# Routed blocks of 64 tokens: both halves of the hidden layer in one tile

## Chip, core and metric

The kernel runs on one NeuronCore of a Trainium2 chip. Times are device microseconds of one execution. The engines are named as in the profile: PE (TensorE matmuls), PEld (TensorE weight loads), DVE (VectorE), ACT (ScalarE), POOL (GpSimd) and SP (SyncE, which issues most DMAs).

## What is computed

The reference is one decoder layer on 2 x 2048 tokens of 512 channels: an attention with squared ReLU, a cross attention with 16 heads on a context of 128 tokens, and a feed-forward layer with a shared expert and 32 routed experts. Only the routed experts matter here. Every token goes to the expert with the largest gate logit, scaled by that logit's sigmoid:

```python
order = jnp.argsort(topk_ids)
sorted_x = xs[order]
g = _grouped_mm(sorted_x, routed_gate_w, tokens_per_expert)
u = _grouped_mm(sorted_x, routed_up_w, tokens_per_expert)
d = _grouped_mm(jax.nn.silu(g) * u, routed_down_w, tokens_per_expert)
```

Each expert has weights of 512 x 1024 for `g` and `u` and 1024 x 512 for `d`, all in float32.

## The kernel before

Every float32 operand is split into two parts, `hi` on ACT (a cast to fp32r, line 93) and `lo` on DVE (the difference, line 96), and products are made as three terms, lo x hi, hi x lo and hi x hi.

The stage `routed` runs from about 1866 us to the end. The experts are ranked by their number of tokens, and each rank has a capacity, `CAP`: 448, 384, five of 256, four of 192, thirteen of 128, eight of 64. Each is cut into blocks of 256, 128 and 64 tokens; this makes 13 blocks of 64. The experts run in groups: a large one, then one of 64 tokens and one of 128, later two of 128. Between them stand blocks of `Rest`, which is a part of the shared expert (lines 823 to 856).

`load` brings one matrix of an expert in eight pieces of 128 x 512 (`raw`), and splits each into `rh` (ACT) and `rl` (DVE). The pieces of `g` and `u` take turns in 48 buffers, those of `d` in 16. So a piece of a later expert can be split only when PE has done with the piece whose buffer it takes.

A block goes through these steps. `gather` fetches its rows (an indirect DMA of POOL, line 905). `turn` transposes them on PE (tile `pt`) and splits them (`th`, `tl`). `gate` and `up` make the products `g` and `u`. `turn_h` transposes the hidden layer (tile `ht`) and splits it (`th`, `tl`). `down` multiplies by `d` and adds the rows to the output with an indirect DMA (line 1019). The steps of neighbouring blocks are interleaved: a block's `turn_h` comes between the next block's `gate` and `up`, and its `down` comes after that `up`.

A block of 64 tokens has only 64 rows. Its turned input holds hi in columns 0 to 63 and lo in columns 64 to 127 of the same tile, so that one matmul gives the hi terms in partitions 0 to 63 of PSUM and the lo terms in partitions 64 to 127. `both` adds the two halves: ACT copies one of them to SBUF, DVE adds the other (lines 952 and 953). The hidden layer has 1024 columns, which are made in two halves of 512 (`n` = 0 and 1 in `up_product`). Each half of each block has an `s` tile of its own, of which the first 64 partitions are used. The product `s<-u,s` is made by POOL (line 969), and `turned` transposes each half in four pieces of 64 x 128 into a PSUM bank of its own (line 912).

The order of the instructions on each engine isn't written out: a planner with estimated durations and priorities orders them when the kernel is built, and every engine then runs its list in that order. PSUM banks come in four pairs; `g` uses P2, `u` P3, `ht` P4, `d` and `pt` P1.

Of the kernel before, what the change touches and what calls it, by code (L numbers as in the profile page):

```python
# [9 lines left out]
FR = mybir.dt.float32r  # L10
# [4 lines left out]
A = mybir.AluOpType  # L15
AF = mybir.ActivationFunctionType
# [6 lines left out]
C = 512  # L23
# [17 lines left out]
def f32(ap):  # L41
    return ap.bitcast(F32)
# [45 lines left out]
def split(g, hi, lo, src, lo_engine=None, hi_engine=None):  # L88

    if isinstance(lo_engine, cycle):  # L90
        lo_engine = next(lo_engine)
    if hi_engine is None:
        g.nc.scalar.copy(hi, src)  # L93
    else:
        hi_engine.tensor_copy(hi, src)
    (lo_engine or g.nc.vector).tensor_tensor(lo, src, f32(hi), A.subtract)  # L96
# [65 lines left out]
def three(terms):  # L162

    (wh, wl), (xh, xl) = terms
    return (wl, xh), (wh, xl), (wh, xh)
# [694 lines left out]
def routed(g, xs, rest, plan, idx, wg, wu, wd, out):  # L860
    nc = g.nc
# [8 lines left out]
    X, S, HT, W = {}, {}, {}, {}  # L870
# [38 lines left out]
    def turned(x, m, bank, tags):  # L909

        for k in range(4):
            nc.tensor.transpose(bank[:, k * m:(k + 1) * m], x[0:m, k * 128:(k + 1) * 128], g.ident[0:m, 0:m])
        hi = g.tile(tags[0], "th", FR, (128, 4, 128))
        if m == 64:
            split(g, hi[:, :, 0:64], hi[:, :, 64:128], bank[:, 0:256].rearrange("p (k n) -> p k n", k=4))
            return (hi,)
        lo = g.tile(tags[1], "tl", FR, (128, 4, 128))
        split(g, hi[:], lo[:], bank[:].rearrange("p (k n) -> p k n", k=4))
        return hi, lo
# [16 lines left out]
    def product(p, x, w):  # L936
        n, last = 0, len(x) * (1 + len(x[0][0])) - 1
        for (xk, k), wk in zip(x, w):
            terms = three((wk, xk)) if len(xk) == 2 else [(v, xk[0]) for v in wk[::-1]]
            for v, y in terms:  # L940
                nc.tensor.matmul(p[:], y[:, k, :], v, start=n == 0, stop=n == last)
                n += 1

    def up_product(b, r, which, tag):
        hi, lo = W[r][which]
        for n in range(2):
            p = g.bank(tag, which)
            product(p, [(X[b], k) for k in range(4)], [(hi[2 * k + n], lo[2 * k + n]) for k in range(4)])
            yield p

    def both(out, p):
        nc.scalar.copy(out, p[64:128])
        nc.vector.tensor_tensor(out, p[0:64], out, A.add)

    def gate(b, r, m):
        S[b] = []
        for p in up_product(b, r, "g", "P2"):
            s = g.tile("G", "s")
            if m == 64:
                both(s[0:64], p)  # L960
            nc.scalar.activation(s[0:m], s[0:64] if m == 64 else p[:], AF.Silu)
            S[b].append(s)

    def up(b, r, m):
        for s, p in zip(S[b], up_product(b, r, "u", "P3")):
            if m == 64:
                u = g.tile("D", "u")
                both(u[0:64], p)
                nc.gpsimd.tensor_tensor(s[0:64], u[0:64], s[0:64], A.mult)
            else:  # L970
                nc.vector.tensor_tensor(s[:], p[:], s[:], A.mult)

    def hidden(b, r, part):
        if part == 0:
# [19 lines left out]
            HT[b].append((hh, hl))  # L994

    def turn_h(b, r, m):
        if m < 256:
            HT[b] = [turned(s, m, g.bank("P4", "ht"), "CD") for s in S.pop(b)]

    def down(b, r, m):  # L1000
        h = HT.pop(b)
        hi, lo = W[r]["d"]
        for j in range(-(-m // 128)):
            o = g.bank("P1", "d")
            if m < 256:
                product(o, [(h[k // 4], k % 4) for k in range(8)], list(zip(hi, lo)))
            else:
                n = 0
                for k in range(8):
                    for w, y in three(((hi[k], lo[k]), h[k // 2])):  # L1010
                        nc.tensor.matmul(o[:], y[:, k % 2, j * 128:(j + 1) * 128], w, start=n == 0, stop=n == 23)
                        n += 1
            v = g.tile("I", "v")
            if m == 64:
                both(v[0:64], o)
            else:
                nc.scalar.copy(v[:], o[:])  # L1017
            rows = slice(0, min(m, 128))
            nc.gpsimd.indirect_dma_start(out=out, out_offset=bass.IndirectOffsetOnAxis(ap=idx[rows, b + j:b + j + 1], axis=0),  # L1019
                                         in_=v[rows], in_offset=None, bounds_check=T - 1, oob_is_err=False, compute_op=A.add)  # L1020
# [4 lines left out]
    for r in order:  # L1025
        at = 0
        while at < CAP[r]:
            m = next(m for m in (256, 128, 64) if at + m <= CAP[r])
# [14 lines left out]
    def first(b, r, m):  # L1043
        if r is None:
            rest.gate(b)
        elif m < 256:
            gate(b, r, m)
        else:
            hidden(b, r, 0)

    def second(b, r, m):
        if r is None:
            rest.up(b)
        elif m < 256:
            up(b, r, m)
        else:
            hidden(b, r, 1)

    def third(b, r, m):
        if r is None:  # L1060
            rest.down(b)
        else:
            down(b, r, m)
# [5 lines left out]
    def turn_hidden(b, r, m):  # L1069
        if r is not None:  # L1070
            turn_h(b, r, m)
# [7 lines left out]
    for i, block in enumerate(blocks):  # L1079
        b, r, m = block  # L1080
# [13 lines left out]
        if i > 0:  # L1094
            third(*blocks[i - 1])
            r = blocks[i - 1][1]
# [136 lines left out]
```

## Time and profile before

| what | value |
|---|---|
| median of 3 runs | 2747.65 us (2745.44 to 2748.27) |
| the profiled execution | 2744.97 us, of which the span is 2743.2 us |
| granted clock of TensorE | 0.997 |
| PE busy in the span | 2681.9 us |
| DVE, ACT, POOL busy | 2054.2, 1786.0, 1033.7 us |
| `s<-u,s` on POOL (line 969) | 26 instructions, 41.0 us |
| `s<-s` silu of 64 partitions (line 961) | 26 instructions, 16.4 us |
| `ht` transposes of 64 rows (line 912) | 104 instructions in 13 blocks |

A row of the timeline gives the start, the time until the last of the merged instructions ended, the engine, the line, the operation, the tiles (result <- operands), the shape and the number of instructions. Matmuls are pipelined: one that takes 0.39 us by its row can start 0.227 us after the one before it. What PE spends on a piece of work is therefore read from start to start. A row of the waits gives the engine and its tile and line, what it waited for, the sum in us, how often, and the longest.

### The profile page before, as it was taken

The numbers are of one execution on the slowest core, as the hardware profiler recorded it, in microseconds if no ns is written. First come the engines' busy times: TensorE is split into PE (matmuls) and PEld (weight loads), VectorE is DVE, ScalarE is ACT, GpSimd is POOL, SyncE is SP. The second block draws the span as 40 slices with busy tenths as digits, with TensorE's granted clock in tenths as the row PEclk, the third lists the DMA queues.
The fourth block names the chain that finished last, engine by engine and source line by source line (L and its number), as shares of the span: only waits on it lengthen the run. The fifth ranks groups of instructions, "written<-read, shape, count | busy, mean of one in ns | idle before, by whom it ended". The sixth has DMA issues, their size and how long they took to land. (4 is left out here: it accounts for less than half of the span.)

```text
span 2743.2 us, 47449 instructions
## 1 busy us (share of the span) xinstructions
PE 2681.9 (98%) x14788; PEld 2293.6 (84%) x14788; DVE 2054.2 (75%) x4671; ACT 1786.0 (65%) x3995; POOL 1033.7 (38%) x821
## 2 busy tenths in 40 slices
PE   7999999999999999999999999999999999999998
PEld 5877877777878999899997888888889888898886
DVE  8888788888887888888876722243777787778985
ACT  6777777787867777777775111133666676768885
POOL 5686566667653333333330030001223122223331
PEclk9999999999999999999999999999999999999999
DMA  4021112112120222322246222254888999899994
GB/s 141 32 70 70 70 62 72 64 58 81 36 70 33 75 90 90 114 78 91 74 138 207 96 93 101 72 173 109 271 265 277 284 302 298 280 279 287 325 316 140
DMA packets 237999, 396.69 MB, mean 145 GB/s; under 512 B 29376, under 2 KB 67280, under 8 KB 237744
## 3 DMA queue, kind: packets, MB, share of 16 engines
q1 hardware_dynamic: 223024, 366.45, 39.5%
q0 software_dynamic: 14720, 27.19, 5.0%
q8 instruction: 117, 1.92, 0.3%
q14 instruction: 138, 1.13, 0.1%
HBM read 311.67 MB, written 83.83 MB: 144 GB/s over the span
## 5 line engine op out<-in xcount | busy, mean ns | idle before, releaser
L96 DVE TENSOR_TENSOR rl<-raw,rh 128x512 fp32r<-128x512 f32 x768 | 510.5, 711 | 106.2 <-ACT rh L93 98.0
L93 ACT CAST rh<-raw 128x512 fp32r<-128x512 f32 x768 | 440.3, 622 | 135.7 <-DMA raw<-in_rg 82.8
L96 POOL TENSOR_TENSOR pl<-p,ph 128x512 fp32r<-128x512 f32 x320 | 427.4, 1344 | 242.9 <-ACT ph L93 219.0
L343 DVE TENSOR_TENSOR p<-s,rl 128x512 f32<-128x512 f32 x512 | 343.4, 683 | 81.5 <-ACT rl L341 62.0
L93 ACT CAST ph<-p 128x512 fp32r<-128x512 f32 x448 | 277.7, 622 | 153.9 <-DVE p L343 148.3
L341 ACT ACTIVATE rl<-s 128x512 f32<-128x512 f32 x512 | 301.3, 599 | 34.7 <-PE s L337 21.1
L1019 POOL DMA_INDIRECT out_dram<-v,idx x46 | 108.0, 2347 | 424.8 <-ACT v L1017 332.8
L448 ACT ACTIVATE e<-e,nm 128x128 f32<-128x128 f32 x512 | 199.2, 391 | 63.2 <-DVE nm L445 62.8
L451 POOL TENSOR_TENSOR e<-e,ri 128x512 f32<-128x512 f32 x128 | 133.5, 1043 | 245.2 <-DVE ri L449 128.3
L298 PE MATMUL o<-pl,vwh 128*128 128x512 f32 x512 | 208.0, 406 | 11.0 <-DVE pl L96 7.6
L337 PE MATMUL s<-qh,kwl 128*128 128x512 f32 x512 | 207.2, 406 | 7.3 <-DVE p L343 7.0
L337 PE MATMUL s<-qh,kwh 128*128 128x512 f32 x512 | 201.1, 393 | 0.0
L337 PE MATMUL s<-ql,kwh 128*128 128x512 f32 x512 | 201.1, 393 | 0.0
L298 PE MATMUL o<-ph,vwh 128*128 128x512 f32 x512 | 200.7, 392 | 0.0
L298 PE MATMUL o<-ph,vwl 128*128 128x512 f32 x512 | 198.8, 392 | 0.0
L96 DVE TENSOR_TENSOR pl<-p,ph 128x512 fp32r<-128x512 f32 x192 | 185.2, 965 | 16.1 <-ACT ph L93 13.7
L905 POOL DMA_INDIRECT x<-xs,idx x46 | 57.3, 1247 | 312.0 <-DMA raw<-in_rd 171.8
L93 ACT CAST hh<-s 128x512 fp32r<-128x512 f32 x92 | 57.0, 620 | 164.3 <-DVE s L760 117.2
L422 PE MATMUL q<-yh,wql 128*128 128x256 f32 x512 | 149.5, 292 | 2.8 <-DVE v L481 2.6
L422 PE MATMUL q<-yh,wqh 128*128 128x256 f32 x512 | 145.6, 284 | 0.0
L422 PE MATMUL q<-yl,wqh 128*128 128x256 f32 x512 | 145.0, 283 | 0.0
L755 PE MATMUL g<-z,sw 128*128 128x512 f32 x576 | 139.5, 390 | 1.7 <-ACT s L759 1.7
(296 smaller groups left out, 7607.9 us busy)
## 6 DMA issues: line engine op xcount, KB each, us to landing
raw<-in_rg SPq DMA_DIRECT2D x256, 256.0 KB, 5.3
raw<-in_ru SPq DMA_DIRECT2D x256, 256.0 KB, 5.1
raw<-in_rd SPq DMA_DIRECT2D x256, 256.0 KB, 4.7
z<-zT SPq DMA_DIRECT2D x128, 256.0 KB, 5.4
b<-x SPq DMA_DIRECT2D x64, 256.0 KB, 2.6
xt<-in_x SPq DMA_DIRECT2D x32, 256.0 KB, 2.7
x<-xt SPq DMA_DIRECT2D x32, 256.0 KB, 2.0
x<-b SPq DMA_DIRECT2D x32, 256.0 KB, 2.3
```

Source lines behind the costliest of these rows:

```text
L93: g.nc.scalar.copy(hi, src)
L96: (lo_engine or g.nc.vector).tensor_tensor(lo, src, f32(hi), A.subtract)
L298: nc.tensor.matmul(o[:], w, y[:], start=kt == 0 and n == 0, stop=kt == 15 and n == 2)
L337: nc.tensor.matmul(s[:], w, y[:], start=n == 0, stop=n == 2)
L341: m0 = nc.scalar.activation(r[:], s[:], AF.Relu)
L343: m1 = nc.vector.tensor_tensor(p[:], s[:], r[:], A.mult)
L422: nc.tensor.matmul(o[:, i, :], part(w, k, p), y[k // 2][:, k % 2, :], start=n == 0, stop=n == 11)
L448: nc.scalar.activation(e[:, hs], e[:, hs], AF.Exp, bias=nm[:, h:h + 1], scale=0.125, accum_out=su[:, h:h + 1])
L451: nc.gpsimd.tensor_tensor(e4, e4, ri[:].unsqueeze(2).to_broadcast([128, 4, 128]), A.mult)
L755: nc.tensor.matmul(p[:], part(w, k, c), y[k][:], start=n == 0, stop=n == 11)
L905: nc.gpsimd.indirect_dma_start(out=x[rows], out_offset=None, in_=xs, in_offset=bass.IndirectOffsetOnAxis(ap=idx[rows, b + j:b + j + 1], ax ...
L1019: nc.gpsimd.indirect_dma_start(out=out, out_offset=bass.IndirectOffsetOnAxis(ap=idx[rows, b + j:b + j + 1], axis=0), in_=v[rows], in_offse ...
```

## The change

For blocks of 64 tokens, the two halves of the hidden layer share one `s` tile: half 0 in partitions 0 to 63, half 1 in partitions 64 to 127. `both` takes the number of the half, and puts its result into those partitions. The silu is made once over 128 partitions after both halves are added. The `u` halves share a tile in the same way, and the product `s<-u,s` is made once, on DVE. `turn_h` transposes the common tile in four pieces of 128 x 128 into one bank. Each result has the first half's tokens in columns 0 to 63 and the second's in columns 64 to 127; two splits take them apart into the same two `th` tiles as before. `down` is the same. Blocks of 128 and 256 tokens do the same work as before, but the planner orders the whole stage anew.

```diff
-    def both(out, p):
-        nc.scalar.copy(out, p[64:128])
-        nc.vector.tensor_tensor(out, p[0:64], out, A.add)
+    def both(out, p, n=0):
+        at, other = slice(64 * n, 64 * n + 64), slice(64 - 64 * n, 128 - 64 * n)
+        nc.scalar.copy(out[at], p[other])
+        nc.vector.tensor_tensor(out[at], p[at], out[at], A.add)

     def gate(b, r, m):
         S[b] = []
-        for p in up_product(b, r, "g", "P2"):
-            s = g.tile("G", "s")
+        for n, p in enumerate(up_product(b, r, "g", "P2")):
             if m == 64:
-                both(s[0:64], p)
-            nc.scalar.activation(s[0:m], s[0:64] if m == 64 else p[:], AF.Silu)
-            S[b].append(s)
+                if n == 0:
+                    S[b].append(g.tile("G", "s"))
+                both(S[b][0], p, n)
+            else:
+                s = g.tile("G", "s")
+                nc.scalar.activation(s[:], p[:], AF.Silu)
+                S[b].append(s)
+        if m == 64:
+            nc.scalar.activation(S[b][0][:], S[b][0][:], AF.Silu)

     def up(b, r, m):
+        if m == 64:
+            u = g.tile("D", "u")
+            for n, p in enumerate(up_product(b, r, "u", "P3")):
+                both(u, p, n)
+            s = S[b][0]
+            nc.vector.tensor_tensor(s[:], u[:], s[:], A.mult)
+            return
         for s, p in zip(S[b], up_product(b, r, "u", "P3")):
-            if m == 64:
-                u = g.tile("D", "u")
-                both(u[0:64], p)
-                nc.gpsimd.tensor_tensor(s[0:64], u[0:64], s[0:64], A.mult)
-            else:
-                nc.vector.tensor_tensor(s[:], p[:], s[:], A.mult)
+            nc.vector.tensor_tensor(s[:], p[:], s[:], A.mult)
...
     def turn_h(b, r, m):
-        if m < 256:
+        if m == 64:
+            s, = S.pop(b)
+            bank = g.bank("P4", "ht", (128, 4, 2, 64))
+            for k in range(4):
+                nc.tensor.transpose(bank[:, k, :, :].rearrange("p n t -> p (n t)"), s[:, k * 128:(k + 1) * 128], g.ident)
+            HT[b] = []
+            for n in range(2):
+                h = g.tile("C", "th", FR, (128, 4, 128))
+                split(g, h[:, :, 0:64], h[:, :, 64:128], bank[:, :, n, :])
+                HT[b].append((h,))
+        elif m == 128:
             HT[b] = [turned(s, m, g.bank("P4", "ht"), "CD") for s in S.pop(b)]
...
             if m == 64:
-                both(v[0:64], o)
+                both(v, o)
```

## The prediction, made before the changed kernel ran

> **What bounds the kernel now.** I read the busy table of the page first, then the busy time by stretches, then what PE waits for in the routed stage, and last its timeline around the transposes that the change touches.
>
> ```profile
> PE 2681.9 (98%) x14788; PEld 2293.6 (84%) x14788; DVE 2054.2 (75%) x4671; ACT 1786.0 (65%) x3995; POOL 1033.7 (38%) x821
> 2100.00:2200.00 100.00, 99.54 (x589) 87.96 (x588) 73.32 (x116) 70.31 (x130) 23.15 (x17) 1.00 0.91 283
> 2500.00:2600.00 100.00, 99.70 (x500) 82.73 (x499) 92.09 (x147) 81.71 (x158) 33.77 (x19) 1.00 0.95 308
> ```
>
> The two lower lines are stretches of the routed stage (about 1866 us to the end); their columns are length, then PE, PEld, DVE, ACT, POOL busy, granted clock, DMA share, GB/s. PE is full to half a microsecond in a hundred while the DMA engines are at 0.91 to 0.95, DVE at 73 to 92%. A busy PE could hide waits, so I checked the pace: 512-column matmuls start every 0.227 us and 256-column ones every 0.12 us throughout. The waits put down to PE in the whole routed stage are small:
>
> ```profile
> PE d L941 <- ACT th L93: 1.0, 1, 1.0
> PE g L941 <- ACT th L93: 0.9, 1, 0.9
> PE g L941 <- DVE th L96: 0.7, 2, 0.4
> PE g L986 <- DVE tl L96: 0.7, 1, 0.7
> ```
>
> So in this stage a microsecond of PE work is a microsecond of kernel, unless PE then runs into its suppliers. What the change removes from PE is therefore read from start-to-start distances, not from busy time. Eight transposes of a 64-token block (64 rows in use), four of a full block, both between 512-column products:
>
> ```profile
> 2714.24 0.39 PE L941 MATMUL g<-rh,th 128*128 128x512 f32 x1
> 2714.56 0.71 PE L912 MATMUL ht<-ident,s 64*128 64x64 f32 x8
> ...
> 2715.54 0.39 PE L941 MATMUL u<-rh,tl 128*128 128x512 f32 x1
> 2467.15 0.39 PE L941 MATMUL g<-rh,th 128*128 128x512 f32 x1
> 2467.38 0.60 PE L912 MATMUL pt<-ident,x 128*128 128x128 f32 x4
> ...
> 2468.05 0.40 PE L941 MATMUL u<-rh,th 128*128 128x512 f32 x1
> ```
>
> Each distance holds two normal steps (0.454). The eight small ones cost 2715.54 - 2714.24 - 0.454 = 0.85 us, the four large ones 0.90 - 0.454 = 0.45 us. Four small ones alone cost 0.59 us by the same measure (the `pt` of these blocks), so a small one is about (0.85 - 0.59) / 4 = 0.065 us and going to 64 rows and back about 0.33 us.
>
> **What the Trainium skill says.** "TensorEngine Tiling (Array Packing)", Key Properties: changing the tiling mode, not only the tile, drains TensorE. The trace agrees: 0.33 us for a run of 64-row transposes whatever its length. "SBUF — State Buffer", Who interferes with whom: a DVE instruction with two SBUF inputs and a GpSimd instruction that reads SBUF exclude each other for a whole instruction. The trace agrees:
>
> ```profile
> L96 DVE TENSOR_TENSOR rl<-raw,rh x742: 669/682/2205, 1903.6 to 2727.9; 128x512 fp32r<-128x512 f32 x186
> L969 POOL TENSOR_TENSOR s<-u,s x26: 1279/1624/2275, 1910.9 to 2708.2; 64x512 f32<-64x512 f32 x26
> ```
>
> (min/median/max ns.) The weight splits normally take 682 ns; the 38 of them that overlap one of the 26 POOL products average 1265, so the products cost DVE 38 x 0.58 = 22 us. "VectorE: DVE Perf Modes", Two Vector instructions with no wait between them: an instruction whose operands start in another group of 32 partitions than those before is held until the earlier ones are done. Before, all of them start at partition 0, so no row shows it; I bound it below.
>
> **The change part by part.** There are 13 blocks of 64 tokens.
>
> PE, transposes of the hidden layer. Before: 8 of 64 rows per block; after: 4 of 128 rows, the form that the 128-token blocks use. In the trace 8 of the 13 blocks have one run beside full-row work (0.84 us each), 2 share the 64-row mode with a neighbouring `pt` (1.09 less the 0.59 that `pt` costs anyway: 0.50), 3 are cut into two runs of four (1.18, 1.25 and 1.19). Sum 6.7 + 1.0 + 3.6 = 11.3 us. After: 13 x 0.445 = 5.8. The compiled order shows one `pt` of 64 rows cut in two (three, eight matmuls, one): one more change of mode, +0.33. PE work: **-5.2 us**.
>
> DVE. The `both` additions stay (four per block, 0.68 each). The product `s<-u,s` comes from POOL, once over 128 partitions: +13 x 0.68 = +8.9 us, price of `hl<-s,hh`, which also reads two SBUF tiles. Lost port time returns, -22 us. Changes of start partition: rows run 0.68 long but start 0.60 apart, so a held one loses about 0.08, and four to eight per block make 4 to 8 us; neither end matters for the path, as DVE has 8% free in its fullest stretch. Net 5 to 13 us less.
>
> ACT. Copies stay; one silu of 128 partitions for two of 64: -13 x 0.63 = -8 us, off the path. POOL: -26 products, 41 us busy; gathers and scatters queued behind them go earlier. PE waits for no gather, so I count 0. The two splits per block read PSUM in pieces of 64 now, the same 256 elements: 0 to +0.1 us each on DVE, hidden under PE.
>
> Waits added. The silu now waits for the second addition too; behind it on ACT stand weight casts (`rh`), and PE waits for these. The product on DVE waits for the silu, and the weight splits queue behind it. The compiled order puts the silu by the copies of `u` and the product one to five entries after the last addition, so the silu is done when the product's turn comes: 0, covered by the `u` product of the same block on PE (16 x 0.227 = 3.6 us); up to 0.6 us for a split behind it if not. I paired each weight piece's split on DVE with the first matmul that reads it: nearly everywhere it is ready 5 us or more ahead. The exception is `u` of the 256-token experts: ready 0.1 to 0.6 us ahead at 2150, 2234, 2316 and 2399 us. There the order changes too. Before, DVE and ACT made both halves of that block's turned input (`th`, `tl`) between those splits; after, four of its eight transposes stand ahead, and one cast (0.5 to 0.6 us) and one `tl` (0.6) leave the queue before the weights. PE loses 0.8 to 1.2 us there per round (4.2 us in four rounds, from gaps in its starts). PE comes there no earlier relative to what frees the buffers: the 64-token `down` moves ahead with it. From -4.2 to +2 us in all; I take about a third of the possible gain: **-1.3 us**.
>
> Loads, stores and their order on SP are the same in number. The tail after the last weight load keeps its order (`ht` of the last 64 block, 24 `u`, 16 `d`, eight `ht`, 24 `d`): 0.
>
> Sum -6.5 us. The profiled execution took 2744.97 us (span 2743.2 plus 1.8 around it), 2.7 below the median of the three runs, 2747.65. So 2738.5 against its own time and 2741 against the median.
>
> **The rivals.**
> 1. *PE saves and then waits.* The tight loads follow ACT and DVE, not PE. If in the five rounds with a 256-token expert PE arrives 0.4 us earlier than its suppliers and in the last groups one of the lone waits (0.4 to 1.1 us) grows, 2 to 4 of the 5.2 us are given back: about 2745. For it: margins of 0.1 us. Against: DVE and ACT get lighter.
> 2. *Slower: the second half of the turned hidden layer is late.* In the compiled order its ACT cast and DVE subtraction stand behind weight splits, and in many blocks behind the product of the block between, so `down` becomes eight matmuls, a few of `g`, eight more. PE reaches the second eight 24 x 0.12 + 4 x 0.11 + 14 x 0.227 + 8 x 0.227 + 2 x 0.227 = 8.8 us after the transposes; DVE should have the half after about 2.9 + 0.3 + 0.7 + 0.4 = 4.3 us. It decides once DVE is 4.5 us behind; 2 us past that in eight blocks is +16, less 6: about 2757. Against: DVE is idle a quarter of the time where most of these blocks lie.
> 3. *DVE was worth more than its busy share says.* The 22 us that POOL held from it fall in bursts of about 1.7 us per block. If most of PE's short waits (some 8 us from the gaps in its starts) come from that backlog, 4 us more go: about 2737.
>
> That the change does not do what it says is ruled out: the compiled order shows 52 transposes of 128 x 128 where 104 stood, and 13 products on DVE.
>
> **How the numbers follow.** Forecast 0.60 (own range 2737 to 2744), rival 1 0.27, rival 2 0.08, rival 3 0.05. A measurement tells about 0.2% (5.5 us) from no change, so faster means below 2742.2. The forecast gives about 0.51 of its 0.60 to that side, rival 3 all, a little of rival 1: 0.57. Within 0.2%: 0.09 + 0.26 = 0.35. Slower: 0.08. The range 2734 to 2748 leaves out rival 2 and the ends.
>
> **What would show it.** Right: `ht` of 64 rows gone, each run of four full ones costing 0.45 us between starts; weight splits without values of 2.2 us; POOL 41 us less busy; PE busy some 5 us less, waits no larger. Rival 1: PE work down, waits on `rl`, `th` or `tl` up by the same. Rival 2: PE `d` waiting for DVE `th`. I am wrong if PE's starts around the new transposes cost 0.85 us as before, or if PE's waits grow by over 5 us.

## The result, and the profile after

The changed kernel took 2739.28 us (median of 11 runs, 2737.38 to 2742.28) against 2746.22 us for the kernel before (11 runs, 2742.96 to 2749.73). The ratio is 0.9975, with a 95% interval of 0.9966 to 0.9985: 0.25% faster, or 7 us.

Page and stretches of the changed kernel (columns as before the change):

```profile
PE 2677.5 (98%) x14736; PEld 2291.0 (84%) x14736; DVE 2046.0 (75%) x4684; ACT 1784.7 (65%) x3982; POOL 985.1 (36%) x795
2100.00:2200.00 100.00, 98.68 (x582) 87.33 (x581) 73.84 (x120) 70.80 (x130) 20.50 (x14) 1.00 0.90 280
2500.00:2600.00 100.00, 98.83 (x481) 81.42 (x480) 90.03 (x149) 81.16 (x155) 24.85 (x15) 1.00 0.96 309
```

PE has 52 matmuls fewer and is 4.4 us less busy. POOL is 48.6 us less busy, of which the products are 41. DVE is 8.2 us less busy although it makes 13 products more. But PE has more small gaps in both stretches than before (98.7 and 98.8 us of 100 instead of 99.5 and 99.7).

The timeline of PE at the last 64-token block, and the same measure as in the prediction: 2711.55 - 2710.65 - 0.454 = 0.45 us, where it was 0.85.

```profile
2710.65 0.39 PE L941 MATMUL g<-rh,th 128*128 128x512 f32 x1
2710.88 0.60 PE L1011 MATMUL ht<-ident,s 128*128 128x128 f32 x4
2711.23 0.48 PE L941 MATMUL u<-rl,th 128*128 128x512 f32 x1
2711.55 0.40 PE L941 MATMUL u<-rh,tl 128*128 128x512 f32 x1
```

The weight splits and the product, by their tiles (min/median/max ns): the 2.2 us splits are gone.

```profile
L96 DVE TENSOR_TENSOR rl<-raw,rh x742: 670/685/735, 1904.9 to 2723.9; 128x512 fp32r<-128x512 f32 x186
L978 DVE TENSOR_TENSOR s<-u,s x13: 684/687/693, 1914.5 to 2704.0; 128x512 f32<-128x512 f32 x13
```

What PE waited for in the routed stage, to be set against the four lines of the prediction:

```profile
PE g L996 <- DVE tl L96: 1.2, 4, 0.3
PE g L996 <- ACT th L93: 1.1, 2, 0.9
PE d L941 <- ACT th L93: 1.0, 1, 1.0
PE d L852 <- DVE tl L96: 0.9, 1, 0.9
```

None of these rows names a weight piece, and none does in the kernel before. PE waits for turned tiles (`th`, `tl`), which stand among the weight splits in the queues of ACT and DVE.

For all kernels I split the routed stage in the same way, from the start of the first `pt` of line 931 to the start of the last matmul. **Products** are all matmuls but the transposes, at their normal distance (0.227 us for 512 columns, 0.1195 for 256): 821.3 us in every kernel. **Transposes** are what each run of them adds from start to start, the change of mode and the restart included. The **rest** is PE waiting, and 1.2 to 1.8 us by which the normal distances are taken too short. Waits that fall into a run of transposes are counted with the run: 1.9 us in the tail of every kernel (the last run of eight takes 2.8 us, others take 0.88), 1.0 us more in the kernel before, 0.5 in e1, 0.7 in e2 and under 0.3 in the others (e8 stands apart). Where an expectation below puts the 1.9 us of the tail into the rest, that is a slip.

Each row is one profiled execution; the ratio is that of the timed runs to the kernel before, with its interval. The two can differ: by its stage e8 is 0.3 us slower than before, by its ratio 3.8. A difference of one or two us in the rest of two executions is therefore not sure.

| kernel | stage us | transposes us | rest us | ratio |
|---|---|---|---|---|
| before | 882.75 | 52.75 | 8.66 | 1 |
| changed | 877.40 | 46.66 | 9.41 | 0.9975 (0.9966 to 0.9985) |
| e1_product_dve | 880.65 | 52.21 | 7.11 | 0.9989 (0.9982 to 0.9996) |
| e2_product_pool | 880.37 | 47.02 | 12.01 | 0.9998 (0.9990 to 1.0006) |
| e3_turn_four_times | 887.95 | 63.53 | 3.09 | 1.0017 (1.0011 to 1.0024) |
| e4_turn_64_rows | 873.97 | 47.97 | 4.67 | 0.9966 (0.9953 to 0.9979) |
| e5_full_input_turn | 873.05 | 44.77 | 6.96 | 0.9963 (0.9949 to 0.9976) |
| e6_turn_seven_times | 905.57 | 80.18 | 4.07 | 1.0086 (1.0072 to 1.0100) |
| e7_order_swapped | 872.50 | 46.50 | 4.67 | 0.9962 (0.9948 to 0.9976) |
| e8_turn_later | 883.09 | together 61.8 | | 1.0014 (1.0007 to 1.0020) |
| e9_full_turn_swapped | 872.21 | 44.64 | 6.24 | 0.9959 (0.9946 to 0.9973) |
| e10_before_swapped | 880.27 | 51.15 | 7.80 | 0.9990 (0.9982 to 0.9998) |
| e11_product_dve_swapped | 874.43 | 51.48 | 1.63 | 0.9969 (0.9957 to 0.9981) |
| e12_product_pool_swapped | 873.78 | 46.50 | 5.95 | 0.9977 (0.9970 to 0.9983) |

So the stage became 5.35 us shorter: 6.1 less in the column of transposes, 0.75 more in the rest. With the 1.0 us of waits taken out of the runs, it is 5.1 us less of transposes and 0.25 us less waiting. In the two profiled executions the stages ahead, whose order of instructions is the same on PE, differ by 1.3 us the other way, and so does what follows the last matmul, by 0.6, so the spans differ by only 3.4 us.

### The profile page after: what moved, and what is told of

It is laid out like the page before. It is cut to its first block, busy times and chain, and to the rows that moved or that the text cites. A ratio compares the mean times of both kernels' runs of the same rounds, so it can differ in the third digit from the quotient of the medians.

```text
span 2739.8 us, 47212 instructions
## 1 busy us (share of the span) xinstructions
PE 2677.5 (98%) x14736; PEld 2291.0 (84%) x14736; DVE 2046.0 (75%) x4684; ACT 1784.7 (65%) x3982; POOL 985.1 (36%) x795
## 5 line engine op out<-in xcount | busy, mean ns | idle before, releaser
L96 DVE TENSOR_TENSOR rl<-raw,rh 128x512 fp32r<-128x512 f32 x768 | 489.4, 685 | 101.6 <-ACT rh L93 89.9
L1039 POOL DMA_INDIRECT out_dram<-v,idx x46 | 101.5, 2206 | 435.8 <-ACT v L1037 359.2
```

## Experiments

**The two halves of the change, one at a time.** First the kernel before with only the product moved:

```diff
-                nc.gpsimd.tensor_tensor(s[0:64], u[0:64], s[0:64], A.mult)
+                nc.vector.tensor_tensor(s[0:64], u[0:64], s[0:64], A.mult)
```

> The kernel before with one edit: the two products s<-u,s of a 64-token block are made by DVE, still in two tiles of 64 partitions; transposes as before. Theory (the gain is PE's transposes): PE keeps 104 transposes of 64 rows, so the time stays within 2 us of before (ratio 0.9993 to 1.0007), although POOL loses 26 products (40 us) and no weight split of DVE takes 2.2 us any more. Rival (DVE freed from the shared port gives the gain): 4 to 7 us faster, ratio about 0.998.

Measured: ratio 0.9989; the stage is 2.1 us shorter, 1.55 of it in PE's waits. That lies between the two theories: more than the 2 us of mine, less than the 4 of the rival. Freeing DVE is worth something. Then the changed kernel with the product on POOL:

```diff
-            nc.vector.tensor_tensor(s[:], u[:], s[:], A.mult)
+            for at in (slice(0, 64), slice(64, 128)):
+                nc.gpsimd.tensor_tensor(s[at], u[at], s[at], A.mult)
```

> The changed kernel with one edit: the product is made by POOL again, in two instructions of 64 partitions on the common tile. Theory: the transposes stay at 52 of 128 rows, so it keeps the gain, 5 to 7 us faster than before (ratio 0.9975 to 0.998), with weight splits of up to 2.2 us back in the trace. Rival (shared port): the gain goes, ratio about 1.000.

Measured: ratio 0.9998, which is what the rival said, though the stage is still 2.4 us shorter than before. The reason isn't that the transposes save nothing. They fell to 47.0 us as in the changed kernel; but the rest rose to 12.0 us. The weight splits of the two experiments, first with the product on DVE (e1), then on POOL (e2):

```profile
L96 DVE TENSOR_TENSOR rl<-raw,rh x742: 670/684/755, 1903.5 to 2725.8; 128x512 fp32r<-128x512 f32 x186
```

```profile
L96 DVE TENSOR_TENSOR rl<-raw,rh x742: 670/684/1797, 1905.5 to 2727.5; 128x512 fp32r<-128x512 f32 x186
```

So neither half alone gives the gain of both. With the product on POOL the common tile takes 5.7 us of transposes from PE, and PE waits 3.35 us more; moving the product to DVE then takes 2.6 of the waits away.

Each kernel has a plan of its own, so I compared the order of the matmuls in the traces, by the names of their tiles (a run of `ht` transposes counted as one, some 4830 in all). "Out of order" are those that the longest common order of two kernels leaves out. From e2 to the changed kernel these are 28, from the kernel before to e2 138. So the 2.6 us are the work of the product under nearly one plan, while the 3.35 can come from the new order as well as from PE being earlier.

**More work on PE.** The changed kernel with each block's transposes made four, then seven times:

```diff
-            for k in range(4):
+            for k in 4 * [0, 1, 2, 3]:
                 nc.tensor.transpose(bank[:, k, :, :].rearrange("p n t -> p (n t)"), ...
```

> The changed kernel with the four transposes of each 64-token block's hidden layer made four times over into the same bank: 12 more per block, 156 in all. Theory (PE's work is the kernel's time one for one in this stage): 156 x 0.11 = 17 us more than the changed kernel, so about 10 us slower than before (ratio 1.0037), PE's waits unchanged within 3 us. Rival (PE waits for its weights, and would absorb some work): under 10 us more, ratio at most 1.001.

> The changed kernel with the four transposes of each 64-token block's hidden layer made seven times over: 156 more than with four times, 17 us of PE. Theory A (PE's waits are waits for supplies, and work put on PE is absorbed until they are used up; with four times over they were down to 3.1 us, 1.9 of them in the tail): now one for one, stage 17 us longer than with four times within 1.5 us, ratio to before about 1.008. Theory B (the waits are luck of the plan): they come back to 6 to 10 us, stage 20 to 24 us longer, ratio 1.009 to 1.011.

With four times over, transposes grew by 16.9 us, as counted, but the stage by only 10.55: waits fell from 9.4 to 3.1 us. That lies between the two theories. With seven times over, another 16.65 us of transposes lengthened the stage by 17.6. That is theory A's outcome, within its 1.5 us; waits rose by 1.0. One reading is that PE's work counts one for one only when PE is not waiting anyway. Another is the plan: from the changed kernel to e3 123 matmuls are out of order, and the new order may hold fewer waits. These two runs do not decide between them.

**Only the transposes undone.** The common tile stays, but each half is transposed by itself:

```diff
-            bank = g.bank("P4", "ht", (128, 4, 2, 64))
-            for k in range(4):
-                nc.tensor.transpose(bank[:, k, :, :].rearrange("p n t -> p (n t)"), s[:, k * 128:(k + 1) * 128], g.ident)
             HT[b] = []
             for n in range(2):
+                at = slice(64 * n, 64 * n + 64)
+                bank = g.bank("P4", "ht")
+                for k in range(4):
+                    nc.tensor.transpose(bank[:, k * 64:(k + 1) * 64], s[at, k * 128:(k + 1) * 128], g.ident[at, at])
                 h = g.tile("C", "th", FR, (128, 4, 128))
-                split(g, h[:, :, 0:64], h[:, :, 64:128], bank[:, :, n, :])
+                split(g, h[:, :, 0:64], h[:, :, 64:128], bank[:, 0:256].rearrange("p (k n) -> p k n", k=4))
```

> The changed kernel with only the transposes undone: the common tile stays, silu and product are made once over 128 partitions, but each half is transposed in four pieces of 64 rows into a bank of its own, half 1 from partitions 64 to 127. Theory: 0.85 us per block on PE again instead of 0.45, so back at the time of before within 2 us (ratio 0.9993 to 1.0007), with the mode change of 0.33 us to be seen in PE's starts. Rival (port, or the new order of the plan): keeps the gain, ratio about 0.9975.

Measured: ratio 0.9966, lower than the changed kernel's 0.9975 though the intervals overlap. Both theories missed it, and the timeline of PE shows the first reason:

```profile
2706.51 0.39 PE L941 MATMUL g<-rh,th 128*128 128x512 f32 x1
2706.83 0.47 PE L1014 MATMUL ht<-ident,s 64*128 64x64 f32 x8
2707.23 0.50 PE L941 MATMUL u<-rl,th 128*128 128x512 f32 x1
2707.56 0.39 PE L941 MATMUL u<-rh,tl 128*128 128x512 f32 x1
```

The eight transposes cost 2707.56 - 2706.51 - 0.454 = 0.60 us, not 0.85. In the program the four of the lower half of the partitions stand ahead of the four of the upper half. But PE ran the two fours side by side: in the trace the starts of the eight are 14, 98, 13, 50, 11, 50 and 14 ns apart. Every second one makes a series of 112, 63 and 61 ns, the other four one of 111, 61 and 64, and the eight of the kernel before, all from the lower half, start 112 and then 61 to 63 ns apart. The signals agree: the last transpose of each four tells the other engines that its four are done, and in the trace the signals come with the seventh and eighth start, not with the fourth and eighth. So this edit undid only 1.3 us of the saving of 6.1. The second reason is that the waits are 4.7 us instead of 9.4; of the 4833 matmuls 121 are out of order.

**The order of the plan.** The same instructions as in the changed kernel, traced in another order, so that only the planner's order differs:

```diff
-        if i + 1 < len(blocks):
-            turn_x(*blocks[i + 1])
         if i > 0:
             turn_hidden(*blocks[i - 1])
+        if i + 1 < len(blocks):
+            turn_x(*blocks[i + 1])
```

> The changed kernel with the same instructions in another order of tracing: the hidden layer of the block before is turned ahead of the input of the block after. Theory B (luck of the plan): PE's waits move by 2 us or more from the 9.4 of the changed kernel, transposes staying at 46 to 48 us. Theory A (supplies): waits within 2 us of 9.4.

And with a lower priority for the turning:

```diff
-            turn_h(b, r, m)
+            with later(g, 30):
+                turn_h(b, r, m)
```

> The changed kernel with the same instructions, the turning of every block's hidden layer given a lower priority in the plan (30 places). Theory B (luck of the plan): PE's waits move by 2 us or more from 9.4, either way. Theory A (supplies): within 2 us of 9.4.

Both did what theory B said. Swapped, transposes stay at 46.5 us and waits fall to 4.7: ratio 0.9962. Turned later, the stage is 5.7 us longer than the changed kernel's, ratio 1.0014, slower than before. Its gaps fall into the runs of transposes as well, so my split doesn't part the two; together they are 61.8 us, and with transposes at 46.5 the waits would be about 15. Two rows of its waits:

```profile
PE g L941 <- ACT th L93: 6.3, 3, 2.9
PE d L852 <- DVE v L955: 1.5, 1, 1.5
```

The largest are again for turned tiles that come late in ACT's queue. So one set of instructions gives waits from 4.7 to some 15 us by its order alone; that is a spread of about twice what the whole change is worth. Theory A and B are not rivals: waits are waits for supplies, but how many there are is set by the plan.

**The change under a second plan.** To see what of the change survives another plan, I made the other three kernels with the swapped order too.

> The kernel before with the two turns traced in the swapped order: the second plan's counterpart of the kernel before. Theory (PE's transposes carry the change, waits are the plan's): transposes 52 to 53 us as before, so 5.5 to 6.5 us more than in the changed kernel swapped; if waits too are near 4.7 us as there, the stage is about 878.5 us, ratio to before about 0.9985. Rival (the swap helps only the changed kernel): waits 8 us or more, stage 882 us, ratio 0.9995 or more.

> The kernel before with the product on DVE (as in e1_product_dve) and the turns swapped. If freeing DVE is worth 1.5 to 2.6 us under every plan, the stage is that much shorter than in e10_before_swapped, all of it in waits. If that was the plan's chance, it is within 1 us of it, or longer.

> The changed kernel with the product on POOL (as in e2_product_pool) and the turns swapped. If POOL's product costs 2 to 3 us under every plan, the stage is 874.5 to 875.5 us against 872.5 for the changed kernel swapped, all of it in waits, ratio to before about 0.9970. If that was the plan's chance, within 1 us of 872.5, ratio 0.9962.

The rest per kernel, which is nearly all waits, with transposes in brackets:

| | first plan | swapped |
|---|---|---|
| two tiles, POOL | 8.66 (52.75) | 7.80 (51.15) |
| two tiles, DVE | 7.11 (52.21) | 1.63 (51.48) |
| one tile, POOL | 12.01 (47.02) | 5.95 (46.50) |
| one tile, DVE | 9.41 (46.66) | 4.67 (46.50) |

In all four pairs the common tile takes 4.65 to 5.75 us of transposes (4.4 to 5.4 without the waits in the runs). In all four the product on DVE lowers the waits, by 1.3 to 6.2 us. In three of these pairs (e2 and the changed kernel, e10 and e11, e12 and e7) at most 28 matmuls are out of order, so this is hardly the plan; in the first two the intervals of the timed ratios don't overlap either. In three of four the common tile raises the waits, by 2.3 to 3.35, in one it lowers them by 1.85. There 124 to 170 matmuls are out of order, so what of this is the tile and what the plan is not shown. The common tile's saving on PE stands in every trace. That it gives time, taken alone, is what stage and ratio point to in all four pairs, but in none are the intervals of the two ratios clear of each other.

The whole change is worth 5.35 us of the stage under the first plan and 7.8 under the second. The stages of e10 and e12 lie between their two expectations. What e10 expected of its waits (4.7) was wrong, so part of what the swap gives depends on the rest of the kernel. The 5.8 us between e10 and e11 are more than either expectation of e11, and more than DVE alone explains under the first plan: with the product on DVE and the swapped order, PE waits only in the tail:

```profile
PE d L941 <- ACT th L93: 1.0, 1, 1.0
PE d L941 <- DVE tl L96: 0.4, 1, 0.4
```

**One more edit.** The blocks of 64 tokens still turn their input in 64 rows. Here they gather 128 rows, the last 64 of which are a row of zeros, and turn it in full:

```diff
-            rows = slice(0, min(m, 128))
+            rows = slice(0, 128)
             nc.gpsimd.indirect_dma_start(out=x[rows], ...
...
-            nc.tensor.transpose(bank[:, k * m:(k + 1) * m], x[0:m, k * 128:(k + 1) * 128], g.ident[0:m, 0:m])
+            nc.tensor.transpose(bank[:, k * 128:(k + 1) * 128], x[:, k * 128:(k + 1) * 128], g.ident)
```

> The changed kernel with one more edit: blocks of 64 tokens gather all 128 rows of their list (the last 64 point at a row of zeros) and turn them in four pieces of 128 x 128, so no instruction of the stage uses 64 rows. Theory now (PE's work counts in full, its waits move by 2 to 3 us with each new plan): transposes cost 13 x (0.59 - 0.45) = 1.9 us less, stage 874 to 878 us, ratio to before 0.996 to 0.998. Rival (what is taken from PE turns into waits): transposes down by 1.9 us and waits up by as much, ratio 0.9975 as for the changed kernel.

> The changed kernel with both: blocks of 64 tokens gather and turn all 128 rows, and the hidden layer of the block before is turned ahead of the input of the block after. If the two add up: transposes 44.8 us, waits near 4.7, stage 870 to 872 us, ratio to before 0.9950 to 0.9960. If waits come with each plan by chance: transposes 44.8, waits anywhere from 4 to 10, ratio 0.995 to 0.998.

Both took 1.9 us from the transposes, as counted from the change of mode. The first also has 2.45 us less waiting than the changed kernel, ratio 0.9963. With the swap the ratio is 0.9959, the lowest of all (median 2734.93 us against 2745.40), but its waits are 6.2 and not 4.7, so the two don't add up. From e7 to e9 only 11 matmuls are out of order: here, under nearly one plan, 1.9 us less of transposes came with 1.6 us more waiting. The interval of e9 overlaps those of e4, e5, e7, e11 and e12, and by a little that of the changed kernel; which of them is fastest is not settled.

## Why the prediction was right

The total was right, and so was its largest term, PE's transposes. Two smaller terms were not, and it is in part luck that they did not show in the total.

- *PE's transposes, -5.2 us:* measured -5.1 for the whole change under this plan and -4.4 under the second, without the waits in the runs. (With them it is -6.1: four single transposes of the kernel before, each followed by a wait for `tl`, took 0.36 us where one alone takes 0.11.) The run of four costs 0.45 us as said. Where a 64-row `pt` stands beside it, the pair costs 0.98 instead of the 1.03 that I added up. The cut `pt` did pay a second change of mode (0.33 us).
- *"A microsecond of PE work is a microsecond of kernel, unless PE then runs into its suppliers":* the second half of the sentence mattered more than I allowed. What e6 adds to e3 counts in full; of the 16.9 us that e3 adds, 6.3 are missing from the stage, whether absorbed or by its new plan.
- *Waits, -1.3 us:* measured -0.25, with the 1.0 us from the runs counted as waits. Here a step failed. I had put the 4.2 us that PE loses at four 256-token experts down to late weights. The weights of these experts did get more margin (by the same pairing, 1.1 to 1.8 us where it was 0.1 to 0.6). But the gaps in PE's starts there are 4.6 us now. They are not waits for weights, and were not before, as the weight loads of PE at the first of the four places show, before and after (in brackets the idle time and what ended it):

```profile
2147.05 0.19 PEld L986 LDWEIGHTS g<-th,rl 128*128 128x128 f32 x1 [0.53 <-ACT th L93]
2148.51 0.19 PEld L986 LDWEIGHTS u<-th,rl 128*128 128x128 f32 x1 [0.33 <-DVE s L971]
2149.71 0.19 PEld L986 LDWEIGHTS g<-tl,rh 128*128 128x128 f32 x1 [0.22 <-DVE tl L96]
```

```profile
2143.84 0.19 PEld L996 LDWEIGHTS u<-th,rl 128*128 128x128 f32 x1 [0.28 <-DVE s L981]
2145.72 0.19 PEld L996 LDWEIGHTS g<-th,rl 128*128 128x128 f32 x1 [1.10 <-ACT th L93]
2148.05 0.19 PEld L996 LDWEIGHTS g<-tl,rh 128*128 128x128 f32 x1 [0.55 <-DVE tl L96]
```

  Both kernels wait there for the two turned tiles, and for the product of an earlier block, which frees the PSUM bank that `u` takes next. In the other places some waits went and others came, such as 1.2 us at 2525.2 and 0.7 at 2635.6, both for a `tl` that the plan now puts late on DVE. I had looked at one place and at one supplier, and not at the plan as a whole.
- *DVE, 5 to 13 us less:* 8.2 less busy; the terms as I listed them come to 5 to 9. The port's 22 us came back nearly in full (the mean of the 742 weight splits fell from 711 to 685 ns, 20 us). But for the path I counted nothing of it, as DVE has 8% free in its fullest stretch, and that step failed: with the product on DVE the stage is 1.3 to 5.8 us shorter in all four pairs. PE waits for single pieces of DVE's queue, and a free share on average does not say when those come.
- *Rival 1 and rival 3* fit what was seen under the first plan: with the common tile come 2.3 to 3.35 us more of waiting, with the freed DVE 1.55 to 2.6 less. They nearly cancel, which is why the total came out near the sum; nothing in the prediction made them cancel. Rival 2, the late second half, did not show: no wait of `d` on `th` beyond the one in the tail.
- The sum of -6.5 us stands against -5.35 in the stage and -6.9 in the medians. The measured gain lies in the range that I gave the forecast itself. But e7 and e8 show that the plan alone could have moved it by 5 us either way: the own range of 2737 to 2744 was narrower than what can be known without the plan's effect.

## What to carry to other kernels

Where PE is full, count what an edit takes from it from start to start, changes of row mode included, since busy times hide them. Then expect a few microseconds either way from the new order alone: when a planner lays out the queues, compare a small edit under at least two orders before believing its size. An elementwise product on a POOL that is mostly idle can still cost time, through the DVE instructions that it holds up.

## What the hardware showed that I had not expected

Transposes of 64 rows from the two halves of the partitions ran side by side, although the program has the four of one half behind the four of the other: eight cost 0.60 us, those from one half alone 0.85.

A DVE instruction whose operands start in the upper half of the partitions, next to ones that start in the lower, lost the overlap with its neighbours. DVE in the changed kernel; the second `s<-g,s` starts at partition 64:

```profile
2695.03 0.69 DVE L96 TENSOR_TENSOR rl<-raw,rh 128x512 fp32r<-128x512 f32 x1
2695.64 0.68 DVE L955 TENSOR_TENSOR s<-g,s 64x512 f32<-64x512 f32 x1
2696.24 1.28 DVE L96 TENSOR_TENSOR rl<-raw,rh 128x512 fp32r<-128x512 f32 x2
2697.55 0.69 DVE L955 TENSOR_TENSOR s<-g,s 64x512 f32<-64x512 f32 x1
2698.27 0.69 DVE L96 TENSOR_TENSOR rl<-raw,rh 128x512 fp32r<-128x512 f32 x1
```

The first addition starts 0.61 us after the instruction ahead of it, 0.08 before that ends. The second starts 0.03 after the end of the one ahead, and so does the one behind it. Behind all 26 additions in the upper half the next instruction starts 31 to 34 ns after their end; in the kernel before, it starts 71 to 79 ns ahead of the end wherever DVE doesn't wait. About 0.106 us are lost at each change, four times per block: 52 x 0.106 = 5.5 us of DVE, within the 4 to 8 that I had bounded.
